# First image's attention: three key tiles of eight converted by DMA, VectorE and ScalarE in the written order, other work dealt one by one

## The chip, the cores and the metric

The kernel runs on one core of one Trainium2 chip. The metric is the device time of one execution in microseconds (us), and the time of a version is the median of several runs. The engines are called PE (TensorE: matmul; its weight loads are PEld), DVE (VectorE), ACT (ScalarE), POOL (GpSimd) and SP (SyncE, which here only issues DMAs).

## The reference

The input x has 8 images of 512 channels and 32 x 32 positions (1024 tokens). Two attention layers follow each other; each adds its result to its input.

```
layer 0:  h = group_norm(x);  q, k, v = w_qkv h + b          # 8 heads of 64 channels
          q, k, v = fake_quant(q), fake_quant(k), fake_quant(v)   # 8 bit, one scale for the whole tensor
          w = softmax(q^T k / 8);  a = w v;  x = x + w_proj a + b
layer 1:  h = group_norm(x);  q, k, v = wq h, wk h, wv h (+ b)    # one head of 512 channels
          x = x + wp (softmax(q k^T / sqrt(512)) v) + b
```

The scales of fake_quant are taken over all 8 images, so q, k and v of all images must be known before the first attention can start.

## The kernel before, in words

**Two phases.** The first phase (to about 585 us) normalises every image, multiplies by the qkv weights, stores q, k and v to DRAM and keeps their extremes. From these come the scales. The second phase takes one image after the other: attention of layer 0, its projection, and layer 1. While PE works on layer 1 of image b, the attention of image b+1 is woven in. The first image has no layer 1 to be woven into, so its attention runs alone, with one companion: `fold` (line 1702), which multiplies layer 1's weights together once (wq with wk into `wa`, wv with wp into `wm`), in 32 products of 128 x 128 by 512 and some small steps.

**The attention of layer 0** (`attention`, line 987). A unit u is one key tile of 128 keys, for one pair of heads and one half of 512 queries: 8 key tiles (s), 2 halves (hf), 4 pairs (j), so 64 units an image. `scores(u)` (line 1001) multiplies two heads' keys by queries into a pair of PSUM banks, of which there are two (`ps_s`), and has ACT take the exponential into `pt` (128 x 1024, f32). `split(u)` (line 1029) cuts `pt` into two f16 halves in a tile `two` of which there are six: the high half is a conversion of `pt` (a "cast"), the low half the remainder `pt - high`, which DVE computes in `rest`. `over_keys` (line 1064) multiplies both halves by the values v into the bank `av`, `totals` (line 1089) by ones into the bank `sm`. In the first image the key tiles 3 and 7 are not cut: they are multiplied in f32 (`plain`, tile `aside`). `need(u)` makes sure that a unit's remainder is written into the program before it is used.

Who casts, before the change: key tiles 2 and 6 POOL, key tile 5 DVE, key tiles 0, 1 and 4 ACT.

**The order of the work.** The loop of `attention` (line 1175 and on) takes four units a turn. A turn that starts at unit u runs, for PE: scores of u+6 and u+7, over_keys and totals of u and u+1, scores of u+8 and u+9, over_keys and totals of u+2 and u+3; split of u+6 and u+7 is written before the scores of u+8, split of u+8 and u+9 at the end. PE's matmuls are chained in the order in which they are written (`mm`, line 202). For DVE and ACT there is a wrapper, `InOrder` (line 72). In its "planned" state it keeps a model of the engines' times, holds back small work as chores, and chains each engine's instructions in the order in which they are written. Outside of it, as in the whole attention of the first image, instructions of DVE and ACT are only placed behind the last planned one, and the compiler's scheduler orders them.

**Dealt work.** Outside of the planned state, side work is put in the list `dealt` with a unit from which it may run, and each `split` takes one piece out (`deal`, line 918); `settle(name)` runs all pieces of a name. Dealt are the quantising steps of the next pair (`load_pair`, line 933: two DVE steps each for q, k and v, and a third for v in f32), the fetch of v, and the division by the row sums (`finish`, line 1108: `spread` inverts the sums and sends them through DRAM to all partitions, `divide` multiplies). The loads of q and k are issued on SP when a pair begins; v is fetched into q's buffer (two buffers `raw`).

**The fold's pace.** Nine steps of `fold` run before the first score product (line 1817), then one step at each odd unit of the first image (line 1008). A step is one product (or a small one). Inside `fold`, `through` (line 1719) is DVE work: four multiply-and-sum passes of 128 x 512 and five small operations; it runs at the last row block. The sums and differences of the blocks of `wa` and `wm` are written right where the products end, then `wm` is stored to DRAM.

After the first image's 64 units, two more turns (`LEAD`, line 1825) run units of the second image, then the planned state begins with the projection (`project`).

Of the kernel before, what the change touches and what calls it, by code (L numbers as in the profile page):

```python
# [9 lines left out]
F32 = mybir.dt.float32  # L10
# [8 lines left out]
P = 128  # L19
# [39 lines left out]
def attn_pair_kernel(  # L59
# [12 lines left out]
    class InOrder:  # L72
# [1 line left out]

        planned = False

        def __init__(self, engine):
            self.engine, self.last, self.t, self.chores = engine, None, 0.0, []  # L80
# [6 lines left out]
        def __getattr__(self, name):  # L87
            op = getattr(self.engine, name)

            def call(*args, **kw):  # L90
                ins = self.latest = op(*args, **kw).ins  # L91
                if InOrder.planned:
                    if name == "dma_start":
                        self.t = max(self.t, pe.t) + 0.5
                    if self.last is not None:
                        tc.add_manual_dep(ins, self.last.name, IN_ORDER, reason="order")
                    self.last = ins
                elif self.last is not None:
                    tc.add_manual_dep(ins, self.last.name, IN_ORDER, reason="order")

            return call
# [204 lines left out]
    with ExitStack() as fast:  # L306
# [611 lines left out]
        def deal(u):  # L918
            i = next((i for i, (at, *_) in enumerate(dealt) if at <= u), None)
            if i is not None:  # L920
                dealt.pop(i)[2]()

        def settle(what):
            while True:
# [4 lines left out]
            dve.settle(what)  # L929

        ao = {}

        def load_pair(b, j, u=None):

            nm = f"{b}_{j}"
            raws = []

            def fetch(i, src):
                if (b, j, i) == (0, 0, 2):
                    raw = aop.tile([P, NH, 512], F32, tag="ao", name="raw_first").rearrange(  # L940
                        "p h n -> p (h n)"
                    )
                else:
                    raw = raw_p.tile([P, T], F32, tag="raw", name=f"raw_{nm}_{i}")
                nc.sync.dma_start(
                    raw if i < 2 else raw.rearrange("p (t d) -> p t d", t=NT), src
                )
                raws.append(raw)

            def whole(raw, _, i):  # L950
                quant2(raw.rearrange("p (t d) -> p t d", t=NT)[:, 3::4, :], vfs[j], i)

            fetch(0, q_d[b][j])
            fetch(1, k_d[b][j])
            qt = qkp.tile([P, T], BF, tag="q", name=f"q_{nm}")
            kt = qkp.tile([P, T], BF, tag="k", name=f"k_{nm}")
            vt = qkp.tile([P, NT, P], F16, tag="v", name=f"v_{nm}")
            todo = (qt, kt, vt.rearrange("p t d -> p (t d)"))

            if b == 0:  # L960
                vfs[j] = xp.tile([P, 2, 256], F32, tag="x", name=f"vf_{nm}")[:, :, 0:P]

            def quants(i):
                for step in (quant, quant2, *([whole] if i == 2 and b == 0 else [])):
                    name, work = "qk" if i < 2 else "qv", lambda step=step: step(raws[i], todo[i], i)
                    if u is None or InOrder.planned:
                        dve.later(name, 0.7, work, pe.t + 12.0, 45.0)
                    else:
                        dealt.append((u + (10 if i < 2 else 18), name, work))

            def fetch_v():
                if len(raws) == 2:
                    fetch(2, v_d[b][:, :, bass.ts(j, P)])
                quants(2)

            if (b, j) == (0, 0):
                fetch(2, v_d[b][:, :, bass.ts(j, P)])
            quants(0)
            quants(1)
            if u is None or InOrder.planned:  # L980
                dve.later("qk", 0.0, fetch_v)
            else:
                dealt.append((u + 10, "qk", fetch_v))
            return qt, kt, vt


        def attention():

# [4 lines left out]
                     for s in range(NT)]  # L993
            pairs = {}
            pairs[0, 0] = load_pair(0, 0)
            pts, parts, avs, sms, rss, ready = {}, {}, {}, {}, {}, {}
            st_free, at_hand = [0.0, 0.0], set()

            aside = l2p.tile([P, 3, NT // 2, 256], F32, tag="vsum", name="aside")
# [1 line left out]
            def scores(u):  # L1001
                b, j, hf, s = units[u]
                if hf == 0 and s == 0:
                    settle("qk")
                nm = f"{b}_{j}_{hf}"
                qt, kt, _ = pairs[b, j]
                st = pair_ps(f"st_{nm}_{s}")
                if b == 0 and u % 2 == 1:
                    next(folding, None)
                awaits(st_free[-2])  # L1010
                for i, r in enumerate(HALF):
                    mm(
                        st[:, i, :], lhsT=kt[r, bass.ts(s, P)],
                        rhs=qt[r, bass.ts(hf, 512)], start=True, stop=True,
                    )
                if u >= 4:
                    need(u - 4)
                if plain(b, s):
                    pt = aside[:, u // 4 % 3].rearrange("p (i k) n -> p i (k n)", i=2)
                else:  # L1020
                    pt = ptp.tile([P, 2, 512], F32, tag="p", name=f"pt_{nm}_{s}")
                there = act.do(
                    1.12, lambda: act.activation(pt, st, AF.Exp, scale=esc),
                    max(pe.t + 0.25, ready.get(u - 4, 0.0) + 0.1),
                )
                st_free.append(there)
                pts[u] = pt, there

            def split(u):

                b, j, hf, s = units[u]
                pt, there = pts.pop(u)
                if not InOrder.planned:
                    deal(u)
                if plain(b, s):
                    parts[u], ready[u] = pt, there
# [4 lines left out]
                def rest():  # L1041
                    dve.tensor_tensor(two[:, 1], pt, two[:, 0], ALU.subtract)
                    ready[u] = dve.t

                def cast(copy=act.copy):
                    at_hand.add(u)
                    copy(two[:, 0], pt)  # L1047
                    done_at = act.t if copy == act.copy else there + 1.5
                    dve.later("sum", elements(1024), rest, done_at + 0.1, 9.0)

                if s % 4 == 2:
                    cast(nc.gpsimd.tensor_copy)
                elif not InOrder.planned and s == 5:
                    cast(dve.tensor_copy)
                else:
                    act.later("cast", 1.02, cast, there, 7.0)

            def need(u):

                while u not in ready:  # L1060
                    e, name = (act, "cast") if u not in at_hand else (dve, "sum")
                    e.begin(next(i for i, c in enumerate(e.chores) if c[0] == name))
# [45 lines left out]
            def finish(b, j, hf, u):  # L1108
# [30 lines left out]
                def spread():  # L1139
# [8 lines left out]
                    if InOrder.planned:  # L1148
                        dve.later("ao", elements(1100), divide, dve.t + 7.0, 20.0)
                    else:  # L1150
                        dealt.append((u + 17, "ao", divide))

                if InOrder.planned:
                    dve.later("ao", 0.4, spread, pe.t + 5.0, 8.0)
                else:
                    dealt.append((u + 10, "ao", spread))

            for u in (0, 2, 4):
                for i in (u, u + 1):
# [542 lines left out]
        def fold():  # L1702
# [10 lines left out]

            row = l1p.tile([P, C], F32, tag="acc1", name="gn1_row")
            nc.sync.dma_start(row, vbias[2:3, :].partition_broadcast(P))
            wide = l1p.tile([P, 2, CC, 32], F32, tag="g", name="wide")
            room = l1p.tile([P, C], F32, tag="rs1", name="fold_room")

            def through(i):
                w, _, col = ((NQ1, NK1, V_BQ), (NV1, WP1, V_BV))[i]  # L1720
                z = small.tile([P, CC], F32, tag="z", name=f"z{i}")
                for e in range(CC):
                    dve.tensor_tensor_reduce(
                        room, wn[w][:, e, :], row, 1.0, 0.0, ALU.mult, ALU.add,
                        accum_out=z[:, e : e + 1],
                    )
                dve.tensor_add(z, z, vec[:, col : col + CC])
                widen(wide[:, i], z)

            for i, (rows, lw, rw) in enumerate(((wa_rows, NQ1, NK1), (wm_rows, NV1, WP1))):  # L1730
                for e in range(CC):
# [6 lines left out]
                        if d + 1 < CC:  # L1738
                            yield
                    act.copy(rows(e), ps.rearrange("p (a n) -> p a n", a=2))  # L1740
                    if e == CC - 1:
                        through(i)
                    yield
                dst, w = ((gb, NK1), (ob, WP1))[i]
                by_channel, _ = weigh(
                    bank, room, lambda e, w=w: wn[w][:, e, :], wide[:, i], f"f{i}"
# [3 lines left out]
                if i == 0:  # L1750
                    dve.tensor_copy(dst, tot)
                    a11, a12, a21, a22, s1, s2, s4 = (wa[:, i] for i in range(7))
                    tt(s1, a21, a22, ALU.add)
                    tt(s2, s1, a11, ALU.subtract)
                    tt(a21, a11, a21, ALU.subtract)
                    tt(s4, a12, s2, ALU.subtract)
                    yield
                    load_wp(0, nc.sync.dma_start)
                    load_x2(0, nc.sync.dma_start)
                else:  # L1760
                    dve.tensor_add(dst, tot, vec[:, V_BP : V_BP + CC])
            (m11, m12), (m21, m22), (v1, v2), (v3, v4) = ([t[:, i] for i in range(2)] for t in wm)
            tt(v1, m11, m12, ALU.subtract)
            tt(v2, m22, v1, ALU.subtract)
            tt(v3, m22, m12, ALU.add)
            tt(v4, m21, v2, ALU.subtract)
            for t, dst in zip(wm, wm_d):
                nc.sync.dma_start(dst, t)

        def check_sums():  # L1770

# [45 lines left out]
        folding = fold()  # L1817
        for _ in range(9):
            next(folding)
        while done < 1:  # L1820
            advance()
        for _ in folding:
# [1 line left out]

        for _ in range(LEAD):
            advance()
        for e in (dve, act):
            e.t = pe.t
        InOrder.planned = True
# [367 lines left out]
```

## Time and profile before

| what | value |
|---|---|
| median of 3 runs | 2587.91 us (2587.77 to 2590.59) |
| the profiled execution's own time | 2593.63 us |
| its span, first to last instruction | 2591.8 us |
| busy: PE, DVE, ACT, POOL | 2530.8, 1905.4, 1358.8, 195.6 us |
| mean granted clock of PE | 0.994 |
| first score product, first image | 590.2 us |
| first product of the projection | 725.5 us |
| POOL casts from 590 to 706 us | 16, mean 1615 ns |
| ACT casts from 590 to 706 us | 26, mean 1046 ns |
| DVE casts from 590 to 706 us | 8, mean 789 ns |
| DVE remainders from 590 to 706 us | 48, mean 1400 ns |

How to read it: the change touches only the stretch from 590 to about 725 us, some 5% of the span, so the averages of the whole page say little on it. The answers below are cut to that stretch. In the list of waits each line names the engine and tile that waited, what it waited for, the total, the number of times and the longest. In the timeline each line gives the start, the length, the engine and line, the operation, what it writes and reads, and in brackets the idle time before it and what ended that. Nearly all instructions of DVE and ACT carry line 91, and PE's line 208, since helpers issue them; they are told apart by their tiles.

### The profile page before, as it was taken

What the parts mean: (1) busy time and instruction counts of PE and PEld (TensorE: products, weight loads), DVE (VectorE), ACT (ScalarE), POOL (GpSimd) and SP (SyncE); (2) the same over time, 40 slices, a digit from 0 to 9 for tenths busy, and PEclk for the clock granted to TensorE, in tenths of its full rate; (3) what the DMA queues carried; (4) which work ended last, traced back from release to release, by engine and by line L of the source; (5) the groups of instructions that cost most, each with busy time, mean ns of one, the idle gap of its engine ahead of it and who ended that gap; (6) DMA issues with size and microseconds to landing.
All of it is one profiled execution on the core that took longest, in us unless ns stands there. A gap on an engine that the chain in (4) does not pass through costs nothing.

```text
span 2591.8 us, 38710 instructions
## 1 busy us (share of the span) xinstructions
PE 2530.8 (98%) x15670; PEld 1756.9 (68%) x15670; DVE 1905.4 (74%) x2748; ACT 1358.8 (52%) x1696; POOL 195.6 (8%) x153
## 2 busy tenths in 40 slices
PE   7999999999889999999999999999999999999998
PEld 4788888873237765775677577757756775777787
DVE  6788777669867877777877787778777777775544
ACT  3222222218856675665566566747665665664121
POOL 0000000002210001000100010010001000100000
PEclk9899999999999999999999999999999999999999
DMA  4343333334311232223212331232232123212211
GB/s 168 130 146 136 114 120 121 130 124 137 115 50 54 62 115 98 62 79 111 86 58 73 121 99 58 95 112 65 79 107 99 46 79 122 83 54 82 86 37 39
DMA packets 156013, 243.09 MB, mean 94 GB/s; under 512 B 26544, under 2 KB 93104, under 8 KB 154288
## 3 DMA queue, kind: packets, MB, share of 16 engines
q1 hardware_dynamic: 125264, 182.81, 21.2%
q10 hardware_dynamic: 30560, 57.71, 6.5%
q8 instruction: 125, 2.05, 0.3%
q14 instruction: 64, 0.52, 0.1%
HBM read 153.64 MB, written 86.28 MB: 93 GB/s over the span
## 4 chain that ended last, share of the span: by engine, by line
PE 65%; DVE 3%; ACT 2%; issue 1%; DMA 1%; POOL 0%; ACTq 0%; SPq 0%; DVEq 0%
PE s L208 15%; PE o L208 14%; PE pj L208 9%; PE v2ps L208 7%; PE av L208 7%; PE g L208 6%; PE st L208 4%; PE sm L208 3%; ACT pt L91 1%; DVE acc L91 1%; DVE two L91 1%; DVE h L91 0%; DMA out_dram<-x 0%; DVE kept_u L91 0%; DVE p L91 0%
## 5 line engine op out<-in xcount | busy, mean ns | idle before, releaser
L91 ACT ACTIVATE pt<-st,esc 128x1024 f32<-128x1024 f32 x496 | 528.1, 1114 | 350.6 <-PE st L208 327.2
L91 DVE TENSOR_TENSOR two<-pt,two 128x1024 f16<-128x1024 f32 x496 | 603.9, 1233 | 131.0 <-POOL two L1047 107.3
L91 ACT CAST two<-pt 128x1024 f16<-128x1024 f32 x358 | 362.3, 1055 | 5.3 <-ACT p L91 5.1
L1047 POOL CAST two<-pt 128x1024 f16<-128x1024 f32 x128 | 173.2, 1353 | 1533.2 <-PE sm L208 768.5
L208 PE MATMUL av<-two,v 128*32 128x512 f16 x3968 | 245.8, 382 | 0.7 <-ACT ao L91 0.7
L208 PE MATMUL s<-g,h 128*128 128x256 f32 x1024 | 233.5, 381 | 0.0
L208 PE MATMUL pj<-ao,wp 128*128 128x512 f32 x512 | 223.6, 595 | 0.0
L208 PEld LDWEIGHTS s<-g,h 128*128 128x128 f32 x1024 | 193.4, 190 | 30.5 <-issue 4.3
L91 ACT ACTIVATE u_ring<-qkps,qkbt 128x512 f32<-128x512 f32 x89 | 61.0, 685 | 253.1 <-PE qkps L208 238.3
L208 PE MATMUL st<-q,k 64*128 64x512 bf16 x1024 | 166.6, 384 | 21.6 <-ACT pt L91 16.4
L208 PEld LDWEIGHTS <-v 128*32 128x32 f16 x3968 | 91.9, 96 | 134.4 <-issue 61.9
L208 PE MATMUL s<-g,sums 128*128 128x256 f32 x768 | 178.6, 382 | 0.2 <-DVE p L91 0.2
L208 PEld LDWEIGHTS pj<-ao,wp 128*128 128x128 f32 x512 | 96.3, 190 | 121.1 <-issue 110.9
L208 PE MATMUL o<-p,v 128*128 128x256 f32 x768 | 175.2, 382 | 1.0 <-DVE p L91 1.0
L208 PEld LDWEIGHTS o<-p,v 128*128 128x128 f32 x768 | 144.6, 190 | 26.8 <-issue 5.7
L208 PEld LDWEIGHTS s<-g,sums 128*128 128x128 f32 x768 | 144.8, 190 | 24.2 <-issue 4.1
L208 PEld LDWEIGHTS <-k 64*128 64x128 bf16 x1024 | 35.8, 94 | 159.8 <-issue 158.2
L208 PE MATMUL sm<-two,ones 128*32 128x512 f16 x1984 | 136.8, 381 | 0.0
L208 PE MATMUL qkps<-half,w_low 128*128 128x512 f32 x480 | 132.6, 399 | 1.9 <-DVE half L91 1.9
L208 PE MATMUL qkps<-half,w_high 128*128 128x512 f32 x480 | 134.4, 403 | 0.0
L208 PE MATMUL qkps<-half,w_mix 128*128 128x512 f32 x480 | 132.6, 399 | 0.6 <-DVE half L91 0.6
L208 PE MATMUL g<-h,wa 128*128 128x256 f32 x512 | 120.9, 385 | 1.8 <-DVE h L91 1.8
(221 smaller groups left out, 3832.1 us busy)
## 6 DMA issues: line engine op xcount, KB each, us to landing
rs<-rs_d SPq DMA_DIRECT2D x76, 256.0 KB
x<-in_x_dram SPq DMA_DIRECT2D x32, 512.0 KB
q_d<-wa SPq DMA_DIRECT2D x32, 512.0 KB
k_d<-wa SPq DMA_DIRECT2D x32, 512.0 KB
v_d<-v_ring SPq DMA_DIRECT2D x32, 512.0 KB
raw<-q_d SPq DMA_DIRECT2D x32, 512.0 KB
raw<-k_d SPq DMA_DIRECT2D x32, 512.0 KB
x_d<-h SPq DMA_DIRECT2D x64, 256.0 KB
```

The lines of the kernel that those rows point to most:

```text
L91: ins = self.latest = op(*args, **kw).ins
L208: ins = nc.tensor.matmul(ps, lhsT=lhsT, rhs=rhs, **kw).ins
L1047: copy(two[:, 0], pt)
```

## The change

Key tiles 0, 1 and 4 of the first image are cast by a DMA that POOL issues (a DMA from SBUF to SBUF, f32 to f16); key tile 6 is cast by DVE; key tiles 2 and 5 by ACT. The exponentials of the DMA's tiles go to a new tile `spare` with three places, in the room that `wide` had. The remainder of a tile cast by DMA is put off: it is written when the unit three later is split, or when `need` asks for it. A new state `strict` chains DVE's and ACT's instructions in the written order, from the first image's attention on. The fold takes three steps in eight units in place of four. `through`, the sums of `wa` and `wm` and the stores of `wm` are dealt one piece at a time; `through` is dealt from the first row block on. The quantising steps are dealt at fixed units, one each; v is fetched as soon as q's buffer is free; `spread` is dealt two units later and `divide` three.

```diff
-        planned = False
+        planned = strict = False
...
                     if name == "dma_start":
                         self.t = max(self.t, pe.t) + 0.5
+                if InOrder.planned or InOrder.strict:
                     if self.last is not None:
...
         def deal(u):
             i = next((i for i, (at, *_) in enumerate(dealt) if at <= u), None)
             if i is not None:
                 dealt.pop(i)[2]()
+                if dealt[i : i + 1] and dealt[i][2].__name__ == "fetch_v":
+                    dealt.pop(i)[2]()
...
+        CAST_BY_DMA, CAST_BY_DVE = (0, 1, 4), (6,)
...
-                        dealt.append((u + (10 if i < 2 else 18), name, work))
+                        dealt.append((u + (12, 14, 19)[i] + n, name, work))
+                        if (i, n) == (0, 1):
+                            dealt.append((u + 13, "qk", fetch_v))
...
-            else:
-                dealt.append((u + 10, "qk", fetch_v))
...
+        spare = l1p.tile([P, 7, CC // 2, 256], F32, tag="g", name="spare")
...
-                if b == 0 and u % 2 == 1:
+                if u % 8 in (1, 4, 6):
                     next(folding, None)
...
+                elif b == 0 and s in CAST_BY_DMA:
+                    at = (u // NT * len(CAST_BY_DMA) + CAST_BY_DMA.index(s)) % 3
+                    pt = spare[:, 1 + 2 * at : 3 + 2 * at].rearrange("p i k n -> p i (k n)")
...
                 if not InOrder.planned:
+                    for v in [v for v in put_off if v < u - 2]:
+                        put_off.pop(v)()
                     deal(u)
...
+                if b == 0 and s in CAST_BY_DMA:
+                    nc.gpsimd.dma_start(two[:, 0], pt)
+                    put_off[u] = rest
+                    return
...
-                if s % 4 == 2:
+                if b == 0:
+                    cast(dve.tensor_copy if s in CAST_BY_DVE else act.copy)
+                elif s % 4 == 2:
                     cast(nc.gpsimd.tensor_copy)
...
             def need(u):
 
+                if u in put_off:
+                    put_off.pop(u)()
...
-                        dealt.append((u + 17, "ao", divide))
+                        dealt.append((u + 20, "ao", divide))
...
-                    dealt.append((u + 10, "ao", spread))
+                    dealt.append((u + 12, "ao", spread))
...
-            wide = l1p.tile([P, 2, CC, 32], F32, tag="g", name="wide")
+            wide = spare[:, 0].rearrange("p k n -> p (k n)")[:, 0 : 2 * CC * 32].rearrange(
+                "p (i e n) -> p i e n", i=2, e=CC
+            )
...
                 for e in range(CC):
-                    dve.tensor_tensor_reduce(
+                    dealt.append((0, "fold", lambda e=e: dve.tensor_tensor_reduce(
...
-                    if e == CC - 1:
+                    if e == 0:
                         through(i)
                     yield
+                settle("fold")
...
-                    tt(s1, a21, a22, ALU.add)
...
+                        dealt.append((0, "wa", lambda args=args: tt(*args)))
...
+                dealt.append((0, "wm", lambda args=args: tt(*args)))
+
+            def keep():
+                for t, dst in zip(wm, wm_d):
+                    nc.sync.dma_start(dst, t)
+
+            dealt.append((0, "wm", keep))
...
         for _ in range(9):
             next(folding)
+        InOrder.strict = True
         while done < 1:
             advance()
...
         for _ in range(LEAD):
             advance()
+        settle("wa")
+        settle("wm")
```

More of the change, by code (lines that the diff above doesn't have):

```diff
@@ L963, in quants @@
             def quants(i):
-                for step in (quant, quant2, *([whole] if i == 2 and b == 0 else [])):
+                for n, step in enumerate((quant, quant2, *([whole] if i == 2 and b == 0 else []))):
                     name, work = "qk" if i < 2 else "qv", lambda step=step: step(raws[i], todo[i], i)
@@ L995, in attention @@
             pairs[0, 0] = load_pair(0, 0)
-            pts, parts, avs, sms, rss, ready = {}, {}, {}, {}, {}, {}
+            pts, parts, avs, sms, rss, ready, put_off = {}, {}, {}, {}, {}, {}, {}
             st_free, at_hand = [0.0, 0.0], set()
@@ L1722, in through, with last @@
                 for e in range(CC):
-                    dve.tensor_tensor_reduce(
+                    dealt.append((0, "fold", lambda e=e: dve.tensor_tensor_reduce(
                         room, wn[w][:, e, :], row, 1.0, 0.0, ALU.mult, ALU.add,
                         accum_out=z[:, e : e + 1],
-                    )
-                dve.tensor_add(z, z, vec[:, col : col + CC])
-                widen(wide[:, i], z)
+                    )))
+                def last():
+                    dve.tensor_add(z, z, vec[:, col : col + CC])
+                    widen(wide[:, i], z)
+                dealt.append((0, "fold", last))
             for i, (rows, lw, rw) in enumerate(((wa_rows, NQ1, NK1), (wm_rows, NV1, WP1))):
@@ L1752, in fold @@
                     a11, a12, a21, a22, s1, s2, s4 = (wa[:, i] for i in range(7))
-                    tt(s1, a21, a22, ALU.add)
-                    tt(s2, s1, a11, ALU.subtract)
-                    tt(a21, a11, a21, ALU.subtract)
-                    tt(s4, a12, s2, ALU.subtract)
+                    for args in (
+                        (s1, a21, a22, ALU.add), (s2, s1, a11, ALU.subtract),
+                        (a21, a11, a21, ALU.subtract), (s4, a12, s2, ALU.subtract),
+                    ):
+                        dealt.append((0, "wa", lambda args=args: tt(*args)))
                     yield
@@ L1762, in fold @@
             (m11, m12), (m21, m22), (v1, v2), (v3, v4) = ([t[:, i] for i in range(2)] for t in wm)
[L1763 to L1768, printed above, removed]
+            for args in (
+                (v1, m11, m12, ALU.subtract), (v2, m22, v1, ALU.subtract),
+                (v3, m22, m12, ALU.add), (v4, m21, v2, ALU.subtract),
+            ):
+                dealt.append((0, "wm", lambda args=args: tt(*args)))
[3 more added lines that the diff above has]
+            dealt.append((0, "wm", keep))
         def check_sums():
```

## The prediction

> **What bounds the kernel now.** On the page, PE is busy 98% of the span and holds 65% of the chain that ended last, so time can only come out of a stretch in which TensorE waits or runs at a lowered clock. The change touches one stretch, the first image's attention and the two groups after it. I read the busy times by stretch first: from the first score product to the end of the fold (590 to 684), from there to the last tiles of the first image (703.6), and on to the first projection product (725.5).
>
> ```profile
> 590.20:684.00 93.80, 88.93 (x751) 28.59 (x754) 82.60 (x101) 84.85 (x92) 21.39 (x13) 0.96 0.35 114
> 684.00:703.60 19.60, 15.81 (x186) 5.18 (x179) 17.91 (x20) 18.00 (x20) 4.45 (x3) 1.00 0.35 126
> 703.60:725.50 21.90, 15.46 (x176) 5.05 (x172) 17.87 (x19) 20.66 (x22) 4.96 (x3) 0.92 0.25 74
> ```
>
> The columns are length, busy PE, PEld, DVE, ACT, POOL, granted clock, DMA share, GB/s. PE does 120.2 us of work in 135.3 us; the other 15 are waits. The first stretch is nearly full (the fold's products lie in it), the other two are not: there ACT is busy 18.0 of 19.6 and 20.7 of 21.9. The waits over these 135 us, longest first (total, times, longest):
>
> ```profile
> PE st L208 <- ACT pt L91: 12.4, 13, 2.1
> ...
> ACT pt L91 <- DVE two L91: 5.7, 4, 3.6
> ...
> DVE raw L91 <- DMA raw<-q_d: 3.4, 2, 2.7
> DVE raw L91 <- DMA raw<-v_d: 3.3, 2, 2.2
> ACT pt L91 <- PE st L208: 3.2, 7, 0.8
> ```
>
> TensorE waits for a score bank that an exponential has still to empty; that exponential sometimes waits for a remainder (DVE "two"); and DVE has stood waiting for a load. The timeline shows the one place where all three join:
>
> ```profile
> 652.98 0.75 DVE L91 TENSOR_SCALAR raw<-raw,rcp 128x1024 f32<-128x1024 f32 x1 [2.22 <-DMA raw<-v_d]
> ...
> 656.85 1.11 ACT L91 ACTIVATE pt<-st,esc 128x1024 f32<-128x1024 f32 x1 [3.61 <-DVE two L91]
> ...
> 658.01 0.51 PE L208 MATMUL st<-q,k 64*128 64x512 bf16 x2 [1.79 <-ACT pt L91]
> ```
>
> A quantising step was put ahead of ready remainders and waited 2.22 us for v (issued at 648.39), then 0.74 for q; ACT idled 3.61, PE 1.79, and the granted clock was 0.91 and 0.92 in the slices 650 to 670. By section PE waits 2.7 (590 to 600), 0.4 (to 640), 1.8 (this place), 3.6 (684 to 704), 6.4 (to 726): 14.9, the missing time.
>
> [...]
>
> ```profile
> 642.87 1.88 POOL L1047 CAST two<-pt 128x1024 f16<-128x1024 f32 x1 [5.00 <-ACT pt L91]
> ...
> 643.77 2.06 DVE L91 TENSOR_TENSOR two<-pt,two 128x1024 f16<-128x1024 f32 x1
> ```
>
> A remainder beside a POOL cast took 2.06 us instead of the median 1.22; the mean from 590 to 706 is 1.40. [...] v and q, 512 KB each, three transfers in flight, landed 4.6 us (648.39 to 652.98) and 5.8 us (649.05 to 654.86) after issue. [...]
>
> **The change, part by part.** Durations are of one profiled execution of 2593.63 us (span 2591.8). It stands 5.7 above the median of the runs, so I carry only the difference over.
>
> *Casts.* Of eight key tiles, 0, 1, 4 went to ACT, 2 and 6 to POOL, 5 to DVE; now 0, 1, 4 go by DMA, 2 and 5 to ACT, 6 to DVE. ACT loses one cast per eight, 8 in all, at 0.96 us start to start (the cast that begins at 604.74 is followed at 605.70): 7.7 us. POOL's 16 casts go, and with them the stretch of DVE's remainders: 48 times (1.40 - 1.22) = 8.6 us. Neither is a gain by itself; they lower the rate of the two engines.
>
> *Fold pace.* A fold step costs PE 1.06 us (641.38 to 642.44). Eight tiles with four steps took 641.07 to 654.78 = 13.7 us, so without steps 9.5. At three steps per eight PE needs 12.6, or 1.58 per tile. ACT then needs 8 exponentials at 1.01, 2 casts at 0.96, 2 evictions at 0.48 and a fold copy, 11.5 per eight or 1.44 per tile. DVE: 6 remainders at 1.14, a cast 0.6, half a pair's quantising 2.2, the division and sums 0.8, the fold's share (10.5 us over 64 tiles) 1.3: 11.8 or 1.47 per tile. So PE becomes the limit throughout, where before it was over-full to 684 and idle after. PE's total work is the same, so what counts is which waits vanish:
> - 684 to 704: six steps move in. Of the 3.6 us wait I take 3.0.
> - the stop at 656: its loads are now dealt at fixed tiles (v is fetched at 13 and quantised from 19, some 9 us later, against 4.6 to 5.8 to land). 1.8, and the clock: (8.21 + 10) x 0.085 = 1.5. Sum 3.3.
> - 704 to 726: the last fold step, the weighting and the by-channel products (three times about 1.06) fill part of the 6.4. But ACT stays the limit there (these are tiles of the second image, casts as before) and DVE gets four wm differences (2.7 us). I take 2.0.
> Sum 8.3.
>
> *What it costs.* The written order makes DVE wait at each DMA-fed remainder. Behind it queue the dealt step, the cast of tile 6 and the next remainders; PE's av products wait for these, then the score banks. At 1.58 per tile DVE gets to tile 0's remainder 6.8 us after its exponential ended (three more exponentials 4.7, ACT's cast 0.96, tile 2's remainder 1.13), to tile 1's after 7.0 and tile 4's after 4.9; PE wants them at about 8. So 5 us is covered, and a late tile 4 has slack. Small losses of order: 1.3 us in all, between 0 and 5. The first "through" (3.6 us of DVE at 579 to 584) moves into the first tiles, where DVE idled 2.7 us for q: nothing. POOL's queue holds only these DMAs. On SP, v comes later but due later; the loads of h move from 615 to about 622, needed at 730; the wm stores (4 of 512 KB) move from 650 to 682 into the stretch after 704, after the last reciprocal's transfers, and the second image reads them: nothing. The last division comes after tile 77 as before; its transfers start 2 tiles later and have 5 tiles (9 us) for the 6 us they took (718.48 to about 724): nothing, at worst 2.
> 8.3 - 1.3 = 7.0 us less.
>
> **Rivals.**
> 1. *Even better* (0.12): the initial wait (2.7, clock 0.84) and the waits after 704 also shrink: 12 to 14 us less, about 2575. Against: ACT is busy 20.7 of 21.9 after 704.
> 2. *A wash* (0.23): the order written by hand has VectorE wait for ACT's casts and for POOL's after 704 (1.5 and 1.9 us already there), with lead of about 1 us over PE. Half a microsecond per eight tiles more is 5 us: 2586.
> 3. *Slower* (0.20): the DMA casts land late. The transfers read 12 MB more in 104 us, beside a DMA share of 0.35[...]. PE waits for two groups per eight tiles, 16 in all, each by the landing time less 7 us. At 7.5 us the 8.3 is gone; at 8.2, 16 x 1.2 = 19.2 less 8.3 makes 10.9 more, 2598.8. For it: the 4.6 to 5.8 us of loads. Against: [...] most run with little beside them.
> That the change does not do what it says is small: the order edges are added where they were missing, and the casts are plain.
>
> **Numbers.** The main case has 0.45: 2587.9 - 7.0 = 2581, its own range 2577 to 2582.5. About 0.2%, or 5.2 us, can be told from no change. Faster: 0.45 + 0.12 = 0.57; same 0.23; slower 0.20. The range 2574 to 2598 reaches into both ends and leaves out about 0.06 below and 0.1 above.
>
> **What would show it.** Right: POOL casts gone in the first image and remainders at 1.22; PE waits from 600 to 704 under 3 us and the projection starting near 718 instead of 725.5; fold products up to the end. Wrong: "DVE two <- DMA two" among the long waits, with PE's av products behind it (rival 3); or PE waits for ACT as before (rival 2).

## The result and the profile after

The changed kernel takes 2614.99 us (median of 6 runs, 2613.11 to 2615.74), the kernel before 2589.25 (6 runs on the same chip): ratio 1.0097, 95% interval 1.0084 to 1.011. It is slower by some 25 us where 7 less were forecast. The profiled execution of the changed kernel took 2613.11 us, with a span of 2611.3.

The first phase is untouched, but its end differs between the profiled executions by some 5 us, so stretches are measured from one product: the last "vps <- w_high" of the first phase. From there to the first projection product, before:

```profile
578.70:725.50 146.80, 130.37 (x1126) 43.70 (x1124) 129.21 (x173) 124.84 (x136) 31.20 (x20) 0.97 0.36 116
```

The same stretch after:

```profile
574.30:737.50 163.20, 133.10 (x1127) 42.07 (x1125) 115.95 (x166) 118.08 (x128) 17.24 (x28) 0.93 0.50 130
```

The columns are length, busy PE, PEld, DVE, ACT, POOL, granted clock, DMA share and GB/s. PE does practically the same number of products and the stretch is 16.4 us longer. ACT and DVE have less to do, as forecast (118.1 and 116.0 us in place of 124.8 and 129.2). PE is busy for more microseconds than before (133.1 in place of 130.4), at a lower mean clock, 0.93, and it is idle for 30.1 us of the stretch where it was idle for 16.4. From the projection to the first score product of layer 1 another 7.9 us are lost (107.1 in place of 99.2). From there to the end both versions take 1767 us.

The longest waits of PE and DVE from 585 to 760 us, after:

```profile
DVE two L91 <- ACT two L91: 40.9, 9, 9.5
...
PE st L209 <- DVE k L91: 19.2, 5, 4.9
...
PE st L209 <- ACT pt L91: 3.8, 7, 1.1
...
DVE two L91 <- DMA two<-spare: 2.3, 2, 1.4
```

The wait of before, for a score bank that ACT had still to empty, fell: over 580 to 860 us from 13.9 us to 5.3 (4.1 for exponentials in `pt`, 1.2 for those in `spare`). DVE hardly waits for the transfers (2.3 us in all). In their place PE waits for "k", the quantised keys of the next pair: once at each of the four pair boundaries (613.76, 647.27, 680.58, 712.55) for 4.2 to 4.9 us. (The fifth wait of that line is 0.35 us long.) The timeline shows what DVE did ahead of the first of them:

```profile
608.16 1.22 DVE L91 TENSOR_TENSOR two<-pt,two 128x1024 f16<-128x1024 f32 x1
...
609.29 0.74 DVE L91 TENSOR_SCALAR raw<-raw,rcp 128x1024 f32<-128x1024 f32 x1
609.96 0.68 DVE L91 CAST two<-pt 128x1024 f16<-128x1024 f32 x1
610.67 1.23 DVE L91 TENSOR_TENSOR two<-pt,two 128x1024 f16<-128x1024 f32 x1
611.82 1.22 DVE L91 TENSOR_TENSOR two<-spare,two 128x1024 f16<-128x1024 f32 x1
612.95 0.75 DVE L91 TENSOR_SCALAR k<-raw,bhi 128x1024 bf16<-128x1024 f32 x1
...
613.76 0.61 PE L209 MATMUL st<-q,k 64*128 64x512 bf16 x2 [4.81 <-DVE k L91]
...
614.41 1.11 ACT L91 ACTIVATE spare<-st,esc 128x1024 f32<-128x1024 f32 x1 [4.84 <-PE st L209]
```

DVE never stands still here, and PE has been waiting since 608.95. The load of k has landed; k's last step is simply written behind the remainder of tile 5, the cast and remainder of tile 6 and the put-off remainder of tile 4, none of which PE needs so soon. The step is dealt at unit 15 of the pair, right ahead of the scores of unit 16 that read it. PE stands, so ACT gets no scores for 4.84 us, makes no casts, and DVE then waits for ACT (9.5, 7.2, 7.3 and 4.1 us behind the four waits, 28 of the 40.9 above): one late step empties the whole ring. The next slices show what follows (the granted clock is the third number from the right):

```profile
610.00:620.00 10.00, 6.24 (x30) 1.49 (x30) 3.66 (x5) 2.77 (x3) 1.05 (x2) 0.66 0.53 139
...
640.00:650.00 10.00, 5.76 (x40) 1.64 (x36) 9.60 (x14) 4.74 (x6) 0.53 (x1) 0.84 0.63 162
650.00:660.00 10.00, 10.00 (x85) 2.76 (x84) 3.00 (x4) 7.53 (x9) 1.05 (x2) 0.82 0.36 71
...
680.00:690.00 10.00, 9.42 (x76) 2.79 (x80) 2.75 (x3) 6.35 (x7) 1.05 (x2) 0.83 0.46 107
...
710.00:720.00 10.00, 7.45 (x46) 1.93 (x50) 5.87 (x6) 5.62 (x6) 0.00 (x0) 0.66 0.34 120
```

After each wait the clock falls, to 0.50 for 6.83, 6.83, 3.41 and 6.83 us. The mean of such a slice counts PE's idle time too; in slices of half a microsecond, PE's busy time times the missing clock, an estimate of what that costs, is 2.82 + 3.14 + 1.70 + 2.92 = 10.6 us, on top of the waits.

The second new wait is later, in layer 1's first stretch. The timeline there, after:

```profile
783.76 1.00 DVE L91 TENSOR_TENSOR grstd_b<-grstd_b,vec 128x4 f32<-128x4 f32 x1 [3.43 <-POOL grstd_b L263]
784.79 1.91 DVE L91 TENSOR_SCALAR h<-h,gmean_b,grstd_b 128x512 f32<-128x512 f32 x4
786.63 0.74 DVE L91 TENSOR_SCALAR raw<-raw,rcp 128x1024 f32<-128x1024 f32 x1
787.41 0.75 DVE L91 TENSOR_SCALAR v<-raw,bhi 128x1024 f16<-128x1024 f32 x1
...
788.21 1.90 PE L209 MATMUL av<-two,v 128*32 128x512 f16 x16 [9.32 <-DVE v L91]
```

These are the value steps of the second image's second pair. They are dealt at units 19 and 20 of that pair, which is after the two turns of LEAD. The planned state that follows never takes from the list `dealt`, so the steps stay there until `settle("qv")` writes them at their use, behind the normalisation. DVE waits there for a step of it that POOL computes (3.43 us), and PE waits 9.32 us for v.

### The profile page after: what moved, and what is told of

Its sections match the earlier page's. It is cut to its first block, busy times and chain, and to the rows that moved or that the text cites. A ratio compares the mean times of both kernels' runs of the same rounds, so it can differ in the third digit from the quotient of the medians.

```text
span 2611.3 us, 38716 instructions
## 1 busy us (share of the span) xinstructions
PE 2530.7 (97%) x15670; PEld 1748.5 (67%) x15670; DVE 1895.6 (73%) x2748; ACT 1352.4 (52%) x1688; POOL 181.7 (7%) x161
## 4 chain that ended last, share of the span: by engine, by line
PE 84%; DVE 5%; issue 3%; ACT 2%; DMA 1%; POOL 0%; ACTq 0%; SPq 0%; DVEq 0%; POOLq 0%
PE s L209 15%; PE o L209 13%; PE qkps L209 12%; PE pj L209 8%; PE av L209 8%; PE v2ps L209 7%; PE g L209 6%; PE vps L209 6%; PE st L209 4%; PE sm L209 3%; DVE two L91 2%; ACT pt L91 1%; PE fold L209 1%; DVE h L91 1%; DVE acc L91 1%
## 5 line engine op out<-in xcount | busy, mean ns | idle before, releaser
L91 DVE TENSOR_TENSOR two<-pt,two 128x1024 f16<-128x1024 f32 x472 | 567.1, 1215 | 170.0 <-POOL two L1063 104.8
L91 ACT ACTIVATE pt<-st,esc 128x1024 f32<-128x1024 f32 x472 | 501.6, 1113 | 354.3 <-PE st L209 339.6
L91 ACT CAST two<-pt 128x1024 f16<-128x1024 f32 x350 | 354.7, 1054 | 13.4 <-PE sm L209 8.1
L209 PE MATMUL av<-two,v 128*32 128x512 f16 x3968 | 248.5, 384 | 13.5 <-DVE v L91 11.7
L1063 POOL CAST two<-pt 128x1024 f16<-128x1024 f32 x112 | 146.2, 1306 | 1460.9 <-PE sm L209 775.8
L209 PE MATMUL st<-q,k 64*128 64x512 bf16 x1024 | 163.9, 386 | 31.5 <-DVE k L91 19.2
```

The lines of the kernel that those rows point to most:

```text
L209: ins = nc.tensor.matmul(ps, lhsT=lhsT, rhs=rhs, **kw).ins
```

## The experiments

All times are medians, of 4 runs for e3, e4 and e5, 6 for the change and 12 to 22 for the others; the ratio is to the kernel before, run beside it (its median was between 2589.2 and 2589.9 us). Where two versions are compared by single profiles, the measure is the time from the last "vps" product to the first score product of layer 1, which leaves the varying end of the first phase out: 246.0 us before, 270.3 after.

| run | what is different | us | ratio, 95% interval |
|---|---|---|---|
| the change | | 2614.99 | 1.0097 [1.0084, 1.011] |
| e1_qk_early | change, q and k steps four units earlier | 2587.2 | 0.9991 [0.9982, 1.0] |
| e10_half_way | change, q and k steps two units earlier | 2588.52 | 0.9992 [0.9985, 0.9999] |
| e2_no_chain | change, without the chain on DVE and ACT | 2594.41 | 1.0019 [1.0011, 1.0028] |
| e3_old_casts | change, casts as before | 2617.4 | 1.0111 [1.0095, 1.0128] |
| e4_before_chain | kernel before, chain alone added | 2602.47 | 1.0047 [1.003, 1.0064] |
| e5_v_handed | change, left value steps handed to the planner | 2612.06 | 1.0082 [1.006, 1.0103] |
| e6_both | e1 and e5 together | 2582.06 | 0.9974 [0.9966, 0.9982] |
| e7_both_old_casts | e6, casts as before | 2590.6 | 1.0002 [0.9993, 1.0011] |
| e8_both_old_pace | e6, a fold step at each odd unit | 2591.11 | 1.0005 [0.9996, 1.0014] |
| e12_both_no_chain | e6, without the chain | 2592.74 | 1.0009 [1.0003, 1.0015] |
| e9_both_ao | e6, `spread` and `divide` where they were before | 2589.42 | 0.9998 [0.9989, 1.0007] |
| e11_both_ao_wm | e9, `wm` sums handed to the planner | 2589.52 | 0.9995 [0.9987, 1.0004] |

**The key steps earlier (e1_qk_early).** The theory: a place in the written order, not a slow engine, costs the 19 us.

```diff
-                        dealt.append((u + (12, 14, 19)[i] + n, name, work))
+                        dealt.append((u + (8, 10, 19)[i] + n, name, work))
                         if (i, n) == (0, 1):
-                            dealt.append((u + 13, "qk", fetch_v))
+                            dealt.append((u + 9, "qk", fetch_v))
```

> The changed kernel with the quantising steps of q and k dealt four units earlier (8 and 10 after the pair's start in place of 12 and 14) and v fetched at 9 in place of 13; all else as changed. Theory A (late key: the last key step stands behind tile 7's turn in VectorE's order, so that the first score product of each pair waits some 4.7 us, four times, and TensorE's clock falls after it): the four waits on k go, 19 us, and some 8 us of lowered clock with them; about 20 to 27 us below the changed kernel, near the kernel before. The wait of 9.3 us for v after the first projection stays, since the differences of wm still take the turns there. Theory B (DMA casts are what costs): no change, within 3 us of the changed kernel. Theory C (chaining as such): within 5 us of the changed kernel.

27.8 us less than the change, with nothing taken out: the same instructions, the q and k steps of each pair (and v's fetch) written four units earlier. PE's longest waits from 580 to 860 us in this version:

```profile
PE av L209 <- DVE v L91: 11.7, 4, 9.4
PE st L209 <- ACT pt L91: 5.0, 9, 1.1
PE pj L209 <- DVE ao L91: 2.1, 1, 2.1
```

The wait for k went from 19.2 to 0.3 us, and from 580 to 750 the clock is at 1.00 in every slice of 10 us. The stretch from the last "vps" product to the projection, in this version:

```profile
573.80:709.40 135.60, 123.47 (x1126) 40.63 (x1124) 115.72 (x166) 117.11 (x128) 18.11 (x28) 1.00 0.60 157
```

It is 27.6 us shorter than in the changed kernel: 9.6 of it are busy PE, which is the clock (10.6 by the sum above), and 18.0 are idle PE, which is the 18.8 of the four waits for k less some longer waits for exponentials. The cause is shown. The value wait is unchanged.

**Only two units earlier (e10_half_way).** Two places, 10 and 12, between the change and e1 (v fetched at 11), to see how far the steps must move.

> The changed kernel with q and k dealt two units earlier only (10 and 12) and v fetched at 11: half the step of e1. In VectorE's order the key's last step now stands ahead of one cast and two remainders (0.7 + 1.2 + 1.2 = 3.1 us) of the pair's last tiles. Theory A: each of the four waits falls from 4.7 us by some 3 to about 1.6 or less, and the clock stays up; 15 to 22 us below the changed kernel, between it and e1, much nearer to e1. Rival (the early keys help because the loads of the next pair start sooner, whatever the place of the key's step): half the gain of e1, about 14 us below.

k is not waited for (0.3 us), and the time is that of e1: the expectation that a part of the wait remains was wrong, and so was the rival, that half the shift gives half the gain. What counts is to be written ahead of the group "cast 6, remainder 6, put-off remainder 4"; the two places tried ahead of it, two units apart, are worth the same.

**Without the chain (e2_no_chain).**

```diff
-        InOrder.strict = True
+        InOrder.strict = False
```

> The changed kernel without the chain of VectorE's and ScalarE's instructions in the first image's attention (the strict state is never entered); casts by DMA, dealing and fold pace as changed. The scheduler now puts the key steps some seven instructions ahead of the pair's end. Theory A: no wait on k; 20 us or more below the changed kernel. Theory B: as slow as the changed kernel. Theory C (the chain as such costs): 20 us or more below too; it parts from A in e1 and in e4.

The scheduler places k's step by itself, and k's waits are gone (0.3 us); 20.6 us come back. The price is in PE's list, first line:

```profile
PE av L209 <- DVE two L91: 12.9, 9, 3.0
```

So the loss needs both the late place and the chain that enforces it.

**The old casts (e3_old_casts).** Rival 3 of the forecast, late transfers, tested by taking the transfers away.

```diff
-        CAST_BY_DMA, CAST_BY_DVE = (0, 1, 4), (6,)
+        CAST_BY_DMA, CAST_BY_DVE = (), (5,)
...
-                    cast(dve.tensor_copy if s in CAST_BY_DVE else act.copy)
+                    cast(dve.tensor_copy if s in CAST_BY_DVE else nc.gpsimd.tensor_copy if s % 4 == 2 else act.copy)
```

> The changed kernel with the casts of the kernel before (tiles 2 and 6 by POOL, 5 by VectorE, 0, 1 and 4 by ScalarE; no DMA); chain, dealing and fold pace as changed. Theory A: the waits on k stay at four times 4 to 5 us; within 8 us of the changed kernel. Theory B: the loss goes, 20 us or more below it.

No faster (2617.4), with k's wait at 23.3 us: the transfers are not the cause. How they land is in the list for the tile "two", after, 585 to 760 us:

```profile
L1057 POOL DMA_DIRECT2D two<-spare x24: 527/527/859, 587.8 to 703.4; - x24
L91 DVE TENSOR_TENSOR two<-spare,two x24: 1216/1219/1227, 592.7 to 710.6; 128x1024 f16<-128x1024 f32 x24
...
DMA to landing us min/median/max: 2.8/3.3/8.4
```

**The chain alone (e4_before_chain).** The kernel before, with DVE and ACT chained from the first score product on as in the change, and nothing else.

```diff
-        planned = False
+        planned = strict = False
...
+                if InOrder.planned or InOrder.strict:
                     if self.last is not None:
...
             next(folding)
+        InOrder.strict = True
```

> The kernel before with the chain alone: VectorE and ScalarE in the written order from the first image's attention on; casts, fold pace and dealing as before (q, k from 10, v from 18). Theory A: the key's last step is written two units earlier than in the changed kernel, so little or no wait on k; within 8 us of the kernel before, where VectorE's waits for POOL's casts can cost some. Theory C: 15 us or more above the kernel before. Theory B: the same as the kernel before.

13.0 us slower than the kernel before beside it (2589.46), between what theories A and C expected. PE's list:

```profile
PE st L209 <- ACT pt L91: 12.0, 16, 1.7
PE wt_f L209 <- DVE wide L91: 6.3, 2, 4.5
PE st L209 <- DVE k L91: 5.4, 4, 2.4
```

With the old places the chain meets `through` (the wait for `wide`), written late, and again k. A chain makes each written place binding; every place that was harmless under the scheduler has to be looked at.

**The left value steps (e5_v_handed).** They are taken from `dealt` and given to the planner when its state begins.

```diff
         InOrder.planned = True
+        for d in [d for d in dealt if d[1] == "qv"]:
+            dealt.remove(d)
+            dve.later("qv", 0.7, d[2], pe.t + 12.0, 45.0)
```

> The changed kernel with one thing more: when the planned state begins, the v steps of the second image's second pair that are still in the dealt list are handed to the planner as chores. Theory A2 (these steps are in a list that the planned state never deals from, so that they are written only at their use, behind the square root that POOL computes, and TensorE waits 9.3 us for v with its clock falling to 0.6): this wait goes, and with the clock it gives 10 to 13 us: about 2603. The waits on k stay. Rival (the wait only moves to another engine's lateness there, since the layer's norm is bound by VectorE): under 4 us.

The value wait falls from 11.7 to 2.4 us, but only 2.9 us come back in the medians (and 5.1 on top of e1, in e6); the profiles give 4.6 and 5.2. PE then stands a few products later at the normalisation, for "h" (2.0 us, product "g") and for an ACT cast (2.0), which the value wait had covered, and the clock falls there too (0.96 from 740 to 800 us, 0.99 from 800 to 900). So the place of the value steps is shown to cause the wait, but of the time it is the rival that came: most of the wait only moves. The expectation counted the whole of it as gain.

**Both mended (e6_both).** e1 and e5 together, the changed kernel without the two faults.

> Both together: q and k four units earlier, and the left v steps handed to the planner. Theory A with A2: 2575, some 14 us below the kernel before, since what the casts, the chain and the fold's pace were forecast to give (8 us, and 11 by the place of the first projection product in the run with early keys) is no longer eaten. Rival (the gain of the early keys run lies in the stretch only and is given back later in any case): as that run, about 2587.

2582.06 us: faster than the kernel before (0.9974) and than the change, by half of the 14 us that were expected. The same stretch as in the first two views, of this version:

```profile
574.10:709.70 135.60, 123.44 (x1126) 40.70 (x1124) 115.73 (x166) 117.12 (x128) 18.12 (x28) 1.00 0.61 157
```

It is 11.2 us shorter than before: 6.9 of it are busy PE (130.37 to 123.44 for the same products, at a clock of 1.00 in place of 0.97), 4.3 idle PE. Not all of it is kept:

```profile
PE g L209 <- ACT two L91: 3.7, 1, 3.7
PE av L209 <- DVE v L91: 2.3, 3, 1.0
PE pj L209 <- DVE ao L91: 2.0, 1, 2.0
```

These lie behind the projection's start; "g" was waited for just so before, "v" and "ao" are new. To the first score product of layer 1 8.4 us are left.

**The parts of the mended version.** e7, e8 and e12 take the casts, the fold's pace and the chain out of e6, one each, with the edits shown above for the casts and the chain and this one for the pace:

```diff
-                if u % 8 in (1, 4, 6):
+                if u % 2 == 1:
```

> As e6_both with the casts of the kernel before (POOL tiles 2 and 6, VectorE 5, ScalarE 0, 1, 4), chain, pace and dealing as in e6. If the casts by DMA relieve engines that bind, it is 5 us or more above e6_both. If the chain and the pace alone carry the gain, within 2 us of it.

> As e6_both with the fold's pace of the kernel before (one step at each odd unit, four in eight). The forecast put 3 us on the steps that move past 684 us and 2 on those past 704: 3 to 5 us above e6_both. If the pace is worth nothing, within 1.5 us.

> The version with the early key steps and the handed value steps, without the chain on VectorE and ScalarE. Theory (the chain pays once the key steps are early: without it the scheduler leaves remainders late, as in the run that only dropped the chain, where PE waited 12.9 us for them in nine places and the clock stayed up): about 2588 us, 5 to 7 us above the same version with the chain, with PE's waits for DVE two near 12 us and none for k or v above 3. Rival (the chain only costs, as the forecast's 1.3 us of order losses says): 2580 to 2581 us.

*Casts:* 8.5 us slower than e6 (6.8 in the profiles), as the first case of the expectation has it. PE's waits for an exponential rise from 7.1 us (5.9 for `pt`, 1.2 for `spare`) to 9.8, for v from 2.3 to 3.9, for "aside" from 1.3 to 2.5, and the mean granted clock of the runs falls from 0.9956 (e6, 14 runs) to 0.9939 (12 runs), an estimated 4.4 us of the span. The relief of ACT and DVE pays once k is early. While PE stood for k, the same change of casts was worth 2.4 us (e3 against the change), and the intervals of these two overlap.

*Pace:* 9.0 us slower, more than either expectation. Most of it comes from the pace only by a detour. The timeline of that version shows one wait:

```profile
695.63 0.75 DVE L91 TENSOR_SCALAR k<-raw,bhi 128x1024 bf16<-128x1024 f32 x1
...
696.44 1.04 PE L209 MATMUL st<-q,k 64*128 64x512 bf16 x4 [6.08 <-DVE k L91]
```

The fold ends sooner, its four `wm` sums come into the list earlier (679 to 685 us) and take the places in which k of that pair was due: `deal` gives one piece per unit, so k slid to the last unit again. The wait is 6.1 us, and the lowered clock behind it (694.0 to 700.9; 0.70 in the slice 690 to 700) costs an estimated 2.2, which together are 8.3 of the 9.0. What the pace is worth by itself this run cannot tell: while PE stands for k, ACT can catch up in the very stretch in which the pace was to pay.

*Chain:* 10.7 us slower (9 by the ratios, 9.7 in the profiles), beyond what was expected. PE waits 10.6 us for DVE's "two" in seven places (1.7 in two with the chain). The rival, that the chain only costs, falls: with the key steps early it gains some 10 us, where it costs 13 in the kernel before.

**`spread` and `divide` earlier (e9_both_ao, e11_both_ao_wm).** An attempt to remove the 2.0 us at "ao" by undoing their delay, in e11 with the `wm` sums left to the planner as well.

```diff
-                        dealt.append((u + 20, "ao", divide))
+                        dealt.append((u + 17, "ao", divide))
...
-                    dealt.append((u + 12, "ao", spread))
+                    dealt.append((u + 10, "ao", spread))
```

> As e6_both with the division's two steps dealt as in the kernel before (10 and 17 in place of 12 and 20). The projection waits 2.0 us for the last division in all runs with the new places. If that wait is on the path: 1.5 to 3 us below e6_both. If TensorE only waits elsewhere (for ScalarE's exponentials): within 1 us.

> As e9_both_ao, with the differences of wm and their stores kept out of the two turns ahead of the projection: they are handed to the planner and must be done before layer 1 uses them. VectorE is busy 9.9 of 10 us there. If VectorE binds in these turns: 2 to 3 us below e9_both_ao. If it only moves its 2.7 us ahead of the projection's evictions: the same, or up to 2 us above.

Both are 7 us slower than e6; of e9 a gain was expected. The wait at "ao" is 2.0 us in e9 as well, so undoing the delay does not remove it. Without the chain (e2, e12) there is none; what in the chained order makes it was not tried further. DVE's timeline in e9:

```profile
624.44 0.15 DVE L91 COPY gb<-wc_f 128x4 f32<-128x4 f32 x1
628.37 0.17 DVE L91 TENSOR_TENSOR rcs<-apart 128x16 f32<-128x16 f32 x1 [3.77 <-DMA apart<-rs]
```

`spread` is fed by a transfer that had not landed (DMA share 0.98 in the slice 620 to 630), and a chained engine stands for it: PE waits 2.79 us for the remainder behind it (631.83) and runs that slice at 0.83. PE's waits for remainders are 6.0 us in place of 1.7, which with the clock (8.17 x 0.17 = 1.4, an estimate) makes 5.7 of the 7.4. The change's delay of `spread` is right once there is a chain. In e11 the wait at the projection moved from "ao" (0.5 us left) to "h" (1.6) and nothing came of it.

## Why the prediction was wrong

**What failed** is the step "its loads are now dealt at fixed tiles (v is fetched at 13 and quantised from 19 ...)", which booked 3.3 us of gain for the stop at 656. It asked only whether the loads land in time, and only for v. It did not ask what stands ahead of each dealt step in DVE's chained order and when PE reads the result: k's second step at unit 15, its reader at 16. It even listed the pieces, "the dealt step, the cast of tile 6 and the next remainders", but as queued behind a transfer, not as standing ahead of k. So its cost of the written order, 1.3 us with an upper end of 5, left out the wait for k: four waits of 4.2 to 4.9 us, and the clock behind them, are the 27.8 us that e1 got back.

**A second place** was booked at nothing by silence: the value steps that are still in `dealt` when LEAD ends. The wait is 9.3 us; mending it gives back 2.9 to 5.2.

**The casts** went as forecast, step by step. POOL's casts are gone, the remainders are at 1.22 us, DVE and ACT have 13 and 7 us less to do. The landing was counted as 5 us, the author's estimate beside loads that took 4.6 and 5.8; it was 3.3 in the median and 2.8 to 8.4. At the transfers DVE waited 2.3 us in all, and PE's products waited 1.7 us for remainders of any kind, so this part of the 1.3 us of order losses was about right. Rival 3 had the sign, by another cause: e3 refutes it.

**The gain** was there behind the faults: e6 is 0.9974 of before, 6.7 us less (4.7 to 8.8), where the sum said 7.0. That the two agree so well is in part luck, since the make-up was not as forecast. PE's waits behind 684 us fell from 10.0 to 5.2 (e6, 664 to 710 us), near the 5.0 forecast. But e8, with the old pace, has 5.0 there beside its wait for k, so that the fold steps did this is not shown. The clock was mis-sized: 1.5 us were forecast for the slices at 656, while the profile before has three falls in this stretch (596.7, 658.2, 709.4), 1.7 us each, and e6 has none; rival 1 had the first of them in view. In part that is chance of these two executions: the mean clock over all runs is 0.9948 before (33 runs) and 0.9956 in e6 (14), an estimated 2 us of the span.

**The chain** was booked as a cost of order (1.3) and nothing else. It costs 13.0 us alone in the kernel before (e4) and gains 9 to 11 in e6 (e12). Rival 2 named it, "order written by hand", but priced it at half a microsecond per eight tiles.

**The last division** was put at "nothing, at worst 2". PE waited 2.0 us for it, but it does so with the division at its old places too (e9).

**The signs to look for** gave the answer at once: PE's waits from 600 to 704 should have been under 3 us, and the three for k alone in that stretch make 13.9; the projection should have started near 718, and started at 737.5.

## What to carry to other kernels

When an order becomes binding on an engine, list for each piece of side work three things: the place at which it is written, what stands ahead of it there, and when its reader is due. Enough idle time on the engine does not answer that, and a list that deals one piece per step lets new work push a due piece past its reader. Check also who empties such a list when the state that deals from it ends. An engine that stands for a few microseconds in a ring of engines can cost more than its wait: here half as much again by the clock (an estimated 10.6 us on 18.8 of waits).

## What the runs showed of the hardware

How long a wait lowers the clock is not one number here. Waits of PE of 1.79 us (before, 658.01), 2.13 (before, 596.40), 2.37 (e12, 648.14) and 2.79 us (e9, 631.83) were followed by a lowered clock, waits of 2.11 and 2.56 us (e2, 644.51 and 671.93) were not. In the profiles before and after, from 575 to 855 us, the clock falls four and five times, each time to 0.50, and for 3.41 us (before) or one, two or four times as long (after), and within each of the two all falls lie on one grid of that step (before: 596.72, 658.16, 709.36 and 777.63, which are 18, 15 and 20 steps apart; after: 612.58, 646.71, 680.84, 711.56 and 779.83, which are 10, 10, 9 and 20 apart). Two stretches cut along this grid, before:

```profile
654.75:658.16 3.41, 1.62 (x10) 0.58 (x6) 3.30 (x4) 1.31 (x2) 0.00 (x0) 1.00 0.11 44
658.16:661.57 3.41, 3.41 (x28) 1.02 (x26) 3.38 (x5) 2.78 (x4) 1.57 (x1) 0.50 0.21 67
```

And two of the same length in e2:

```profile
643.07:646.49 3.42, 1.98 (x22) 0.78 (x21) 3.42 (x5) 1.87 (x2) 0.00 (x0) 1.00 0.27 50
646.49:649.90 3.41, 3.41 (x34) 0.96 (x34) 2.69 (x3) 2.71 (x4) 0.53 (x1) 1.00 0.64 193
```

The shorter wait (1.79 us) lies within one step, in which PE is busy for 47%; the longer one in e2 (2.11 us, from 642.40) is cut by the edge at 643.07, and PE is busy for 58% of the step that has most of it. In the profiles before and after, of the steps at full clock in which PE was busy for less than 40%, all 6 were followed by a lowered one; between 40 and 60% it was 3 of 10; above 60% none of 132. So in these traces a fall of the clock went with PE's share of a step and not with the length of a wait alone. Executions differ: the mean clock of 38 runs of the kernel before lies between 0.993 and 0.997.

In the changed kernel, with DVE busy 67.3 of 96 us (588 to 684), the issue of a transfer from POOL took 0.53 us and its landing 3.3, both in the median over the 24. The slow transfers came with traffic: leaving out the first two, the 12 with a DMA share of 0.70 or less in the 3 us from their issue landed in 2.8 to 3.6 us, the 10 with 0.81 or more in 3.0 to 8.4, and the slowest (issued at 624.99, share 0.97) beside the 2 MB load of h (issued at 622.65). No run took that traffic away.
